# A graph network on one core: the last 14 groups of the edge layer without early products, and the last store of maxima on ScalarE's queue

## The chip, the cores and the metric

The kernel runs on one core of a Trainium2 chip. The metric is the time of one execution on the device in microseconds; the number for a kernel is the median over its runs. The chip's engines are called as in the profile: PE is TensorE (matrix products), DVE is VectorE, ACT is ScalarE, POOL is GpSimd, SP is the engine that here only issues transfers. ACT and POOL have transfer queues of their own as well. Each engine works through its instructions in a fixed order, and an instruction that waits holds up all that stand behind it on its engine.

## The reference, cut to what matters

12,500 nodes with 32 features each, 400,000 edges sorted by the node they end in (`dst`). Four graph layers follow each other, each with a residual and a layer norm. The third is the edge layer, the fourth the one behind it:

```
edge_index = jnp.stack([src, dst])
x = _layernorm(x + _L0_gnn_ref(x, src, dst, ...))
x = _layernorm(x + _L1_gnn_ref(x, edge_index, 3))
x = _layernorm(x + _L2_gnn_ref(x, edge_index, edge_attr_32, ...))   # the edge layer
x = _layernorm(x + _L3_gnn_ref(x, edge_index))                      # three rounds

# L2: rol, col = edge_index
e_feat = jnp.concatenate([x[rol], x[col], edge_attr], axis=-1)       # 96 per edge
h = jax.nn.relu(e_feat @ W1 + b1)                                    # 64
v = h @ W2 + b2                                                      # 32
x_cand = jax.ops.segment_max(v, col, num_segments=num_nodes)
return jnp.maximum(x_cand, x)

# L3, three times: msgs = norm[:, None] * x[src]; x = segment_sum(msgs, dst, n); acc = acc + x
```

## The kernel before, in words

**Matrix A.** The graph's adjacency lies in device memory as a matrix of small counts, A, in 25 blocks of columns (`NQ`) by 98 blocks of rows (`H`), with what does not fit it in an extra part, Ax. A round of the fourth layer is a product of A and Ax with x, which is split into three 16-bit parts (`x3`). In `Rounds.product` the extra part comes first (its loop value c is -1): two loads of Ax (L363, 3136 KB each), 392 matmuls on them (L377), a scan and a sum, and then the blocks of A (L354 or L363, L382).

**The edge layer** (`edge_layer`) takes the edges that are left for it in three stages, cut by node (`HS` = 52 and 78 of 98 row blocks). A stage is a chain of batches of at most 48 columns of 128 edges; a batch is worked off in groups of four columns. For a group, POOL gathers the rows of its source nodes (`fetch`, L111, four gathers), PE transposes them (L1751), DVE copies the result (L1753) and the indices of a group four further on (L1729, `allow`), PE makes the hidden layer (L1782, L1784, `hidden`), ACT applies relu (L1787), PE makes the outputs (L1800, `outer`; L1806 for the last column, which stands alone), and ACT copies them (L1802, L1808). POOL can run ahead of PE by four groups, for so many index tiles are released. When a batch is through, 32 scans of DVE (L1637) make running maxima, and the SP queue stores them to `scan` (L1640).

**The end of a stage** (`end`, then `done`): PE transposes the flags and the last maxima (L1656, L1659, L1672, L1677), DVE carries the maxima over the partitions (L1657 to L1674), POOL gathers the rows to mend (`fx`, L111), DVE mends them (L1684), POOL scatters them (L116) and then gathers the last row of every node's segment (`ends`, L111, one gather per block of 128 nodes: 20 in the last stage, in batches of eight, eight and four). DVE and ACT make x of each batch out of them (L1309 to L1319, `layernorm` L236 to L245, `split` L254 to L258). These are generators: `tick` takes each one step further per group, `steps` the scans.

**Early products.** As soon as a stage's nodes are done, the products of their rows of A for the first round of the fourth layer are begun (`round_part`): 25 blocks of columns, for each one or more loads of A (L1361, 832 KB), 52 or 26 matmuls (L1366) into one of two buffers `y`, a copy `ys` by ACT (L1373), a sum `z` by PE into the one buffer `z` (L284, placed seven products into the next block), and an addition into `part` by DVE (L1351). `fill` puts eight of them behind each half of a group. The products of the last 20 row blocks are not early; they come in the first round itself (`lo` = 78), behind Ax.

**What sets the order.** A scheduler lays the instructions of each engine in a fixed order, by priority in the order of writing and by when it reckons them ready; it can draw later-written work forward into gaps. Buffers of a pool that is closed are free for the next pool only when their users are through; the first buffer that Ax is loaded to lies where the tiles of A for the early products lay.

Of the kernel before, what the change touches and what calls it, by code (L numbers as in the profile page):

```python
# [22 lines left out]
P = 128  # L23
D = 32
# [96 lines left out]
def dense_path(ctx, tc, bad_i, x, src, dst, edge_attr, w1T, w1_b, w2, w2T, w2_b, aT,  # L121
               m_W1, m_b1, m_W2, m_b2, out):
    nc = tc.nc
# [3 lines left out]
    C = E // P  # L127
# [17 lines left out]
    HE = P * HC  # L145
    ROW = D + 2
    scan = dram.tile([E - HE, D], F32, name="scan")
# [66 lines left out]
    cuts = [HC]  # L214
# [461 lines left out]
    with ExitStack() as build:  # L676
# [15 lines left out]
        for k in (1, 256, 255):  # L692
            t = keys.tile([P, P], BF16, name=f"ident{k}")
# [273 lines left out]
        steps = []  # L967
# [324 lines left out]
    with ExitStack() as st:  # L1292
# [5 lines left out]
        fillers = []  # L1298
# [78 lines left out]

        begun = set()

        def fill(i):  # L1380
            for _ in range(2 - i):
                next(first[0], None)
            if fillers:
                k = 8 if fillers[0] in begun else 40
                begun.add(fillers[0])
                while fillers and k:
                    try:
                        next(fillers[0])
                        k -= 1
                    except StopIteration:  # L1390
                        fillers.pop(0)
# [155 lines left out]
def edge_layer(ctx, tc, ident, cuts, heads, edge_attr, m_W1, m_b1, m_W2, table, scan, starts_d,  # L1547
# [11 lines left out]
    nc = tc.nc  # L1559
    E = edge_attr.shape[0]  # L1560
    C = E // P
    HE = P * cuts[0]
    T = 48
    AHEAD = 4
    LEAD = 2 * AHEAD
    HID = m_W1.shape[1]

    const = ctx.enter_context(tc.tile_pool(name="e_const", bufs=1))
# [3 lines left out]
    def of_stage(ap, s, skip=0):  # L1572
        return ap[P * cuts[s] - skip:P * cuts[s + 1] - skip].rearrange(
            "(p t) d -> p (t d)" if len(ap.shape) == 2 else "(p t) -> p t", p=P)

    rows = const.tile([P, C], I32, name="rows")
    for s in range(len(cuts) - 1):
        nc.sync.dma_start(rows[:, cuts[s]:cuts[s + 1]], of_stage(rows_d, s))
    mw1 = const.tile([3 * D, HID], F32, name="mw1")
    mb1 = const.tile([2 * HID, 1], F32, name="mb1")  # L1580
# [14 lines left out]
    class Batch:  # L1595
# [37 lines left out]
        def maxima(self):  # L1633
            n = self.n
            prev = self.before.o[:, self.before.n - 1, :] if self.before else low
            for f in range(D):
                nc.vector.tensor_tensor_scan(self.o[:, :n, f], self.keepb[:, :n], self.v[:, :n, f],  # L1637
                                             prev[:, f:f + 1], OP.min, OP.max)
                yield
            nc.sync.dma_start(of_stage(scan, self.s, HE)[:, self.t0 * D:(self.t0 + n) * D],  # L1640
                              self.o.rearrange("p t d -> p (t d)")[:, :n * D])
            if self.t0 + n == cuts[self.s + 1] - cuts[self.s]:
                later.append(end(self.s, self.o[:, n - 1, :]))

# [3 lines left out]
    def end(s, last):  # L1648

        cont0, single, fix, _ = heads[s]  # L1650
        g = small.tile([D, P], F32, name="cg", bufs=1)
        a = small.tile([D, P], F32, name="ca", bufs=1)
        b = small.tile([D, P], F32, name="cb", bufs=1)
        c = small.tile([D, P], F32, name="cc", bufs=1)
        pr = scratch()
        nc.tensor.transpose(pr[:D], cont0.to_broadcast([P, D]), ident)  # L1656
        nc.vector.tensor_copy(g, pr[:D])  # L1657
        pr = scratch()
        nc.tensor.transpose(pr[:D], single.to_broadcast([P, D]), ident)  # L1659
        nc.vector.memset(a[:, 0:1], 0.0)  # L1660
        nc.vector.tensor_mul(a[:, 1:], g[:, 1:], pr[:D, :P - 1])
        for r in (g, a):
            nc.vector.tensor_scalar(r, r, -0.5, BIG, op0=OP.add, op1=OP.mult)
            nc.vector.tensor_scalar_mul(r, r, 2.0)
        nc.vector.memset(b[:, 0:1], -BIG)
        if s:
            nc.sync.dma_start(b[:, 0:1], scan[P * cuts[s] - HE - 1:P * cuts[s] - HE, :].rearrange(
                "o d -> d o"))
            nc.vector.tensor_tensor(b[:, 0:1], b[:, 0:1], g[:, 0:1], op=OP.min)
        yield  # L1670
        pf = scratch()
        nc.tensor.transpose(pf[:D], last, ident)  # L1672
        nc.vector.tensor_tensor(b[:, 1:], pf[:D, :P - 1], g[:, 1:], op=OP.min)
        nc.vector.tensor_tensor_scan(c, a, b, -BIG, OP.min, OP.max)  # L1674
        yield
        po = scratch()
        nc.tensor.transpose(po[:, :D], c, ident[:D, :D])  # L1677
        carry = small.tile([P, D], F32, name="carry", bufs=1)
        nc.scalar.copy(carry, po[:, :D])
        yield from range(LEAD)  # L1680
        fx = small.tile([P, D], F32, name="fx", bufs=1)
        gather(nc, fx, scan[:P * cuts[s + 1] - HE], fix)
        yield from range(2)
        nc.vector.tensor_tensor(fx, fx, carry, op=OP.max)  # L1684
        yield
        scatter(nc, scan[:P * cuts[s + 1] - HE], fix, fx)
        yield
        yield from done(s)
# [8 lines left out]
    def batch(i):  # L1697
        s, t0, n = plan[i]
        return Batch(i, s, t0, n, made[-1] if t0 else None)
# [4 lines left out]
    todo = []  # L1704

    def steps(k):
        while todo and k:
            try:
                next(todo[0])
                k -= 1  # L1710
            except StopIteration:
                todo.pop(0)

    def tick():
        for g in list(later):
            try:
                next(g)
            except StopIteration:
                later.remove(g)

    groups = [(cuts[s] + t, min(4, t0 + n - t)) for s, t0, n in plan
              for t in range(t0, t0 + n, 4)]
# [11 lines left out]
    for _ in range(AHEAD):  # L1734
        allow()
    made.append(batch(0))
    for i in range(len(plan)):
        B = made[i]
        for _ in B.ready:
            pass  # L1740
        if i + 1 < len(plan):
            made.append(batch(i + 1))
            todo.append(made[-1].ready)
        for t in range(0, B.n, 4):
            k = min(4, B.n - t)
            for j in range(k):
                B.fetch(t + j)
            allowed.pop(0)
            pT = psum.tile([P, 4, P], F32, name="pT", bufs=2)
            for j in range(k):  # L1750
                nc.tensor.transpose(pT[:3 * D, j, :], B.ef[:, t + j, :], ident)  # L1751
            eT = small.tile([3 * D, 4, P], F32, name="eT")
            behind = nc.vector.tensor_copy(eT[:, :k], pT[:3 * D, :k])  # L1753
            with tc.issue_after(behind.ins):
                allow()
            fill(0)
            stage1.append((B, t, k, eT))
            if len(stage1) > 1:
                stage2.append(hidden(nc, psum, small, mw1, mb1, *stage1.pop(0)))
            if len(stage2) > 1:  # L1760
                ready = stage2.pop(0)
                outer(nc, psum, mw2, *ready)
                if ready[1] + ready[2] == ready[0].n:
                    todo.append(ready[0].maxima())
            fill(1)
            steps(6)
            tick()
    stage2.append(hidden(nc, psum, small, mw1, mb1, *stage1.pop(0)))
    for ready in stage2:
        outer(nc, psum, mw2, *ready)  # L1770
    todo.append(B.maxima())
    steps(10 ** 6)
    while later:
        tick()


def hidden(nc, psum, small, mw1, mb1, B, t, k, eT):
# [691 lines left out]
```

## Time and profile before

| what | us |
| --- | --- |
| median of 9 runs (lowest, highest) | 7677.07 (7664.44, 7686.70) |
| the profiled execution's own time | 7678.94 |
| its span, first to last instruction | 7677.0 |
| PE busy | 6633.4 (86%) |
| DVE busy | 3924.4 (51%) |
| POOL busy | 3575.2 (47%) |
| ACT busy | 1636.3 (21%) |
| early products (L1366, 1950 of them), first to last start | 5586.4 to 6580.6 |
| gathers of the edge layer (`ef`, 2817 of them), last start | 6537.1 |
| gathers of ends of the last stage, first to last start | 6581.9 to 6605.9 |
| products of Ax in the first round (L377, 392 of them), first to last start | 6592.1 to 6638.5 |

Times in views are microseconds from the start of the span. A line of a timeline gives the start, the duration, the engine, the line of the kernel, what is written and read, how often, and in brackets how long the engine stood idle before it and what ended that. "issue" is time in which the profile shows no wait. PE's matmuls are pipelined, so a group's duration reaches a little beyond the start of the next. The granted clock is 1.00 when PE runs at full rate.

### The profile page before, as it was taken

What the parts mean: (1) busy time and instruction counts of PE and PEld (TensorE: products, weight loads), DVE (VectorE), ACT (ScalarE), POOL (GpSimd) and SP (SyncE); (2) the same over time, 40 slices, a digit from 0 to 9 for tenths busy, and PEclk for the clock granted to TensorE, in tenths of its full rate; (3) what the DMA queues carried; (4) which work ended last, traced back from release to release, by engine and by line L of the source; (5) the groups of instructions that cost most, each with busy time, mean ns of one, the idle gap of its engine ahead of it and who ended that gap; (6) DMA issues with size and microseconds to landing.
All of it is one profiled execution on the core that took longest, in us unless ns stands there. A gap on an engine that the chain in (4) does not pass through costs nothing. (4 is left out here: it accounts for less than half of the span.)

```text
span 7677.0 us, 194318 instructions
## 1 busy us (share of the span) xinstructions
PE 6633.4 (86%) x84402; PEld 5276.4 (69%) x84402; DVE 3924.4 (51%) x10962; ACT 1636.3 (21%) x3386; POOL 3575.2 (47%) x3459
## 2 busy tenths in 40 slices
PE   6778999899999988888888888778669979899998
PEld 4678899889999985555545555334335635799998
DVE  6989899561555565555555555433344333411121
ACT  1324688200000002222222222211112212100000
POOL 1002501000665727777777777777777777100000
PEclk7879999999999996777777777555559968999999
DMA  2128544799999982222222222121127735699998
GB/s 51 58 103 326 199 205 196 294 337 368 356 378 358 369 328 75 61 55 59 55 58 61 55 55 59 52 60 49 50 74 226 250 89 183 245 347 365 359 363 311
DMA packets 574338, 1447.42 MB, mean 189 GB/s; under 512 B 108023, under 2 KB 269407, under 8 KB 560031
## 3 DMA queue, kind: packets, MB, share of 16 engines
q1 hardware_dynamic: 432816, 1347.10, 47.6%
q0 software_dynamic: 109792, 66.25, 4.2%
q10 hardware_dynamic: 30864, 21.54, 1.0%
q8 instruction: 664, 10.88, 0.6%
q14 instruction: 202, 1.65, 0.1%
HBM read 1155.33 MB, written 279.27 MB: 187 GB/s over the span
## 5 line engine op out<-in xcount | busy, mean ns | idle before, releaser
L111 POOL DMA_INDIRECT ef<-table,ids x2817 | 2670.6, 948 | 883.9 <-issue 652.8
L382 PE MATMUL y<-x,a 128*128 128x96 bf16 x49980 | 2215.3, 207 | 86.2 <-issue 84.9
L382 PEld LDWEIGHTS <-a 128*128 128x128 fp8e4 x49980 | 2154.9, 98 | 117.4 <-issue 115.3
L1751 PE MATMUL pT<-ident,ef 128*96 128x128 f32 x2817 | 773.2, 356 | 586.2 <-DMA ef<-table,ids 571.0
L1751 PEld LDWEIGHTS pT<-ident,ef 128*96 128x96 f32 x2817 | 396.4, 160 | 1045.2 <-DMA ef<-table,ids 718.4
L1753 DVE COPY eT<-pT 96x512 f32<-96x512 f32 x705 | 476.3, 676 | 1045.6 <-PE pT L1751 1045.5
L1019 PE MATMUL pa<-oh,ol 128*128 128x196 bf16 x4928 | 736.4, 273 | 126.1 <-DVE oh L1009 80.6
L1800 PEld LDWEIGHTS pv<-mw,hT 128*128 128x128 f32 x3208 | 594.3, 259 | 265.1 <-issue 90.2
L1025 ACT ACTIVATE at<-pa 128x784 uint16<-128x784 f32 x816 | 646.9, 824 | 510.8 <-PE pa L1019 482.3
L1800 PE MATMUL pv<-mw,hT 128*128 128x64 f32 x3208 | 674.7, 348 | 22.1 <-ACT hT L1787 15.5
L1787 ACT ACTIVATE hT<-ph,mb 128x256 f32<-128x256 f32 x802 | 380.5, 474 | 1313.7 <-PE ph L1784 1286.3
L1019 PEld LDWEIGHTS <-ol 128*128 128x128 bf16 x4928 | 560.2, 150 | 142.0 <-issue 77.1
L1055 PE MATMUL y<-x,at 128*128 128x102 bf16 x9604 | 640.6, 210 | 9.6 <-DVE x L258 5.4
L1782 PE MATMUL ph<-eT,mw 96*64 96x256 f32 x1410 | 622.3, 534 | 11.7 <-DVE eT L1753 10.3
L278 DVE TENSOR_REDUCE v<-y 128x128 f32<-128x384 f32 (+2 forms) x152 | 83.4, 549 | 1064.4 <-PE y L272 579.5
L1784 PE MATMUL ph<-eT,mw 96*64 96x256 f32 x1408 | 625.1, 537 | 0.0
L1009 DVE TENSOR_TENSOR oh<-bins_h,pl 128x1568 bf16<-128x1568 bf16 x616 | 603.5, 980 | 0.0
L111 POOL DMA_INDIRECT g<-code_d,ws_i x25 | 215.9, 8636 | 808.4 <-DVE ki L793 589.1
L116 POOL DMA_INDIRECT sorted_d<-hrow,pos x308 | 404.3, 1313 | 379.1 <-DVE v L1249 192.3
L1055 PEld LDWEIGHTS <-at 128*128 128x128 fp8e4 x9604 | 556.9, 98 | 22.8 <-issue 11.1
L1366 PE MATMUL y<-a,x 128*96 128x512 fp8e4 (+1 forms) x1950 | 492.8, 389 | 2.3 <-DVE x L258 1.5
L1004 DVE TENSOR_TENSOR ol<-la,lb 128x1024 bf16<-128x1024 bf16 x616 | 428.0, 697 | 70.9 <-PE pa L1019 70.6
(409 smaller groups left out, 6821.4 us busy)
## 6 DMA issues: line engine op xcount, KB each, us to landing
a<-A SPq DMA_DIRECT2D x245, 3136.0 KB
A<-at SPq DMA_DIRECT2D x98, 1568.0 KB
a<-A SPq DMA_DIRECT2D x144, 832.0 KB
ef<-table,ids POOLq DMA_INDIRECT x2817
starts_d<-rows SPq DMA_DIRECT2D x44, 1024.0 KB
attr<-in_edge_attr SPq DMA_DIRECT2D x57, 768.0 KB
begin<-starts_d SPq DMA_DIRECT2D x57, 768.0 KB
scan<-o SPq DMA_DIRECT2D x57, 768.0 KB
```

The lines of the kernel that those rows point to most:

```text
L111: return nc.gpsimd.indirect_dma_start(out=o, out_offset=None, in_=tab, in_offset=IndirectOffsetOnAxis(ap=idx, axis=0))
L382: nc.tensor.matmul(y[:, q, :], block(h, q - q0), x3[:, h, :3 * F], start=(q + h == first), stop=(c >= CX and q == nq - 1 and h == H - 1))
L1009: nc.vector.tensor_tensor(oh, bins_h[:, None].to_broadcast([P, 4, HJ, 2]), pairs(pl[:, t, 0, half * 64 + w0:half * 64 + w0 + 8])[:, :, Non ...
L1019: nc.tensor.matmul(pa[:, 2 * b + i, :HJ], ols[t][:, :, :, 4 * u + 2 * b + i].rearrange("p a b -> p (a b)"), ohs[t][:, 2 * u + b, :, i], st ...
L1025: nc.scalar.activation(at[:, qd, :, off:off + 8].rearrange("p h (w j) -> p h w j", w=4), pa[:, :, :HJ].rearrange("p w (h j) -> p h w j", h ...
L1055: nc.tensor.matmul(y[0][:, q, :], at[:, q - 2 * half, h, :], x3[:, h, :3 * F0], start=(q + h == 0), stop=(not EARLY <= c < CX and last and ...
L1366: nc.tensor.matmul(y[:3 * D, :nq * Q], x3[:, h, :3 * D], a[:, :nq, h - h0, :], start=(h == lo), stop=(h == hi - 1))
L1751: nc.tensor.transpose(pT[:3 * D, j, :], B.ef[:, t + j, :], ident)
L1753: behind = nc.vector.tensor_copy(eT[:, :k], pT[:3 * D, :k])
L1782: nc.tensor.matmul(ph[:HID, :ka], mw1, eT[:, :ka], start=True, stop=True)
L1784: nc.tensor.matmul(ph[HID:2 * HID, :k - 2], mw1, eT[:, 2:k], start=True, stop=True)
L1800: nc.tensor.matmul(pv[:, j].rearrange("p h d -> p (h d)"), hT[:, j, :], mw2, start=True, stop=True)
```

## The change

`fill` gets a second argument and issues early products only where it is not zero. The count of groups that are left is divided by `HOLD` = 14, so in the last 14 groups it is zero. Behind the last group the scans are no longer written in one go, but four at a time with a `fill` between, and so are the steps of `end` and `done`. The store of the very last batch of maxima, and the small load of one row of `scan` at the end of the last stage (L1667), go to ACT's queue in place of SP's.

```
-        def fill(i):
+        def fill(i, left=1):
             for _ in range(2 - i):
                 next(first[0], None)
-            if fillers:
+            if fillers and left:
                 k = 8 if fillers[0] in begun else 40
...
+    HOLD = 14
...
-            nc.sync.dma_start(of_stage(scan, self.s, HE)[:, self.t0 * D:(self.t0 + n) * D],
-                              self.o.rearrange("p t d -> p (t d)")[:, :n * D])
+            end_of_all = self.s == len(cuts) - 2 and self.t0 + n == C - cuts[self.s]
+            (nc.scalar if end_of_all else nc.sync).dma_start(
+                of_stage(scan, self.s, HE)[:, self.t0 * D:(self.t0 + n) * D],
+                self.o.rearrange("p t d -> p (t d)")[:, :n * D])
...
-            nc.sync.dma_start(b[:, 0:1], scan[P * cuts[s] - HE - 1:P * cuts[s] - HE, :].rearrange(
+            (nc.scalar if s == len(cuts) - 2 else nc.sync).dma_start(b[:, 0:1], scan[P * cuts[s] - HE - 1:P * cuts[s] - HE, :].rearrange(
...
+    total = len(groups) + AHEAD
     for i in range(len(plan)):
...
-            fill(0)
+            total -= 1
+            left = total // HOLD
+            fill(0, left)
...
-            fill(1)
+            fill(1, left)
             steps(6)
             tick()
...
     todo.append(B.maxima())
-    steps(10 ** 6)
+    while todo:
+        steps(4)
+        fill(1)
     while later:
         tick()
+        fill(1)
```

Behind `edge_layer`, `while fillers: fill(0)` still writes what is left of the early products, before the rounds begin.

## The prediction

> **What bounds the kernel now.** I read first the busy shares (PE 86%), then the windows around the end of the edge layer, then in the timelines what TensorE (PE), GpSimd (POOL) and the SP queue do there, then the SP queue's waits. The change touches only the stretch from about 6486 us on. Before and after it the order of every engine's instructions stays, but for one small load at 6229 us.
>
> Windows (start:end, length, busy time and count of PE, PEld, DVE, ACT, POOL, then granted clock, DMA share, GB/s):
>
> ```profile
> 6404.00:6487.00 83.00, 83.00 (x492) 52.72 (x490) 26.69 (x103) 17.42 (x40) 58.74 (x63) 1.00 0.69 215
> 6487.00:6538.00 51.00, 51.00 (x304) 32.61 (x303) 15.16 (x58) 10.16 (x24) 34.87 (x37) 1.00 0.69 215
> 6538.00:6581.00 43.00, 42.91 (x254) 27.55 (x252) 11.46 (x52) 7.61 (x19) 1.94 (x3) 1.00 0.60 189
> 6581.00:6592.00 11.00, 0.63 (x4) 0.52 (x4) 0.22 (x1) 0.37 (x1) 7.62 (x9) 0.63 0.91 340
> 6592.00:6619.00 27.00, 9.31 (x94) 8.77 (x94) 14.16 (x48) 2.84 (x9) 11.50 (x12) 0.63 0.58 210
> ```
>
> PE is full until 6581 (early products, L1366, between the groups' work), then nearly idle while POOL gathers the segment ends; DMA loads in that gap. The timelines (start, duration, engine, instruction, count, idle before it and what ended that) of POOL, PE and the SP queue:
>
> ```profile
> 6537.07 0.94 POOL L111 DMA_INDIRECT ef<-table,ids  x1 [0.36 <-DVE ids L1729]
> 6576.00 0.94 POOL L111 DMA_INDIRECT fx<-scan,fix  x1 [37.99 <-DMA a<-A]
> 6579.53 0.98 POOL L116 DMA_INDIRECT scan<-fx,fix  x1 [2.59 <-DVE fx L1684]
> 6581.94 0.96 POOL L111 DMA_INDIRECT ends<-scan,end_i  x1 [1.43 <-DMA scan<-fx,fix]
> ```
>
> ```profile
> 6558.15 0.27 PE L1751 MATMUL pT<-ident,ef 128*96 128x128 f32 x1
> ...
> 6564.36 0.41 PE L1806 MATMUL pv<-mw,hT 64*128 64x32 f32 x2
> ...
> 6565.79 7.09 PE L1366 MATMUL y<-a,x 128*96 128x512 fp8e4 x32
> ...
> 6578.66 2.25 PE L1366 MATMUL y<-a,x 128*96 128x256 fp8e4 x19
> ...
> 6592.12 7.14 PE L377 MATMUL y<-a,x 128*96 128x128 fp8e4 x78 [10.06 <-issue]
> ...
> 6619.07 19.61 PE L377 MATMUL y<-a,x 128*96 128x128 fp8e4 x298 [1.41 <-DVE x L258]
> ```
>
> ```profile
> 6570.82 0.33 SPq L1640 DMA_DIRECT2D scan<-o  x1
> 6572.91 0.37 SPq L1361 DMA_DIRECT2D a<-A  x1
> 6581.05 0.98 SPq L363 DMA_DIRECT2D a<-Ax  x2
> ```
>
> And of the SP queue's waits:
>
> ```profile
> SPq L363 <- PE y L1366: 4.4, 1, 4.4
> ```
>
> To be seen: (1) PE transposes the last column 21 us after POOL gathered it (6537.07, 6558.15): PE carries a backlog. (2) The load of Ax (L363) starts when the last early product has ended (6578.66 + 2.25 = 6580.9; issue 6581.05), and its first product L377 stands 11.2 us behind that end. Today these 11.2 us lie beside the gathers of the ends, for 298 of the 392 products of Ax wait for the last x at 6619.0. They end at 6638.7, and the round behind them cannot start sooner.
>
> **The change, part by part.** I follow one chain: P, the end of the last early product, then the load of Ax, then L377.
>
> *No products in the last 14 groups.* The first group held is transposed at 6485.7. In the changed order 35 of the 298 products left then still stand between the last nine groups, and 263 stand behind t0, the end of the last group's L1806. Before, t0 = 6564.8, with 72 behind it.
> - POOL is freed of its waits for ids. The next gather starts at 6487.40; 36 follow before the last at the pace of 6164 to 6240 (1.249 us each): 6532.3, against 6537.1 (no gain).
> - From there to t0: a landing of 2.4 us (the scatter of 6579.53, its reader at 6581.94). Then, before, 6.6 us from 6558.15 to t0, with 18 products at 0.216 (the row of 32: 6565.79 to 6572.71), 3.9; without them 2.7, with the 7 left 4.2; at half clock twice that, 8.4. The stretch without products, 6200 to 6250, ran at 0.50, one with 5 or 6 per group at 0.72 to 0.74: I take 6. PE's lag there is 0 to 5; I take 2, as from 6200 to 6250 PE was busy for 37.7 of 50 us and POOL waited for nothing. t0 = 6542.8 (6539 to 6548).
>
> *The small load of a column (L1667)* goes from SP to ScalarE's queue around 6229; what it waits for lands by 6229.3 and ScalarE's neighbours stand at 6229.5 and 6231.2: nothing.
>
> *The last store of maxima on ScalarE.* Before, SP issues it at 6570.82, when the 32 scans end at 6570.8: SP held nothing back. On ScalarE's queue a copy ys (L1373) stands ahead of it, which needs 29 products and a z (0.81): 29 x 0.216 + 0.8 + 0.6 = 7.7 us behind t0, against 6.1. So it comes 1.7 us later relative to t0, and with it the gather of fx. TensorE's four transposes of the carry, too, stand behind 53 products and two z: 13.6 us, against 10.6. From t0 to the first gather of ends it was 17.2; I take 20 (17.2 to 22.7, the upper with a landing under load: 6600.91 to 6607.12, 6.2 us).
> The Trainium skill ("Trainium Kernel Development and Optimization", Key Constraints) says that DMAs from all queues share the same 16 DMA engines, and that another issuing engine only saves issue time. By it this edit is worth at most the row's 0.33 us; without the ys copy ahead the sum would be about 1.7 us lower.
>
> *Ends.* 20 gathers: 23.97 from the first's start to the last's (6581.94, 6605.91), and a landing of 2.4 (to 6.2): 26.4. So the last batch lands at 6542.8 + 20 + 26.4 = 6589.2; x is ready 9.3 later (6609.75 to 6619.02), at 6598.5, 20.5 earlier than now.
>
> *A new wait.* In the changed order ScalarE's copy ys of one block of columns stands behind L257 of the first batch of ends, and that (over L256) behind VectorE's L1309 of the third batch, so behind the last gather's landing. z of that block (L284) waits for this ys. PE reaches it 34.8 us behind t0 (140 products 30.3, five z 4.0, four transposes 0.5); the copy ends 46.4 + 2.0 behind t0 (L1309 0.34, L256 0.43, L257 0.41, ys 0.58, gaps). PE stands still for some 13 us, everything queued behind that z: 97 full products, 26 half ones (0.118), five z: 21.0 + 3.1 + 4.0 = 28.1. Resuming cold costs up to 3 (at 6619 the clock is 0.50 for 5.9 us); I take 2.5. P = 6589.2 + 2.0 + 30.6 = 6621.8, against 6580.9.
>
> *Load of Ax, then L377.* Its wait for the last product stays. Nothing covers it now: 11.2 to the first product. 196 of the first half: 65 in 5.9 us at half clock, 131 at 0.05, 12.5; the second half lands 8 us behind the first and takes 9.8. End: 6621.8 + 33.5 = 6655.3, against 6638.7: 16.6 later. The tiles of A behind it come in beside L377, as now, so the rest shifts as a whole.
> The page "TensorE: Matmul & The Clock Gate", Part 1, has the clock released after some 3.4 us of activity. The row says 5.9. By the page both cold starts together would cost about 2 us less, and the sum would be +14.5.
>
> **Sum.** The profiled execution spans 7677.0 us (device time 7678.9, 1.9 above the median 7677.1). Its span plus 16.6 is 7693.6; on the median, 7693.7. With all lower values P = 6539 + 17.2 + 26.4 + 2 + 28.1 = 6612.7, +7.5; with all upper ones 6548.2 + 22.7 + 30.2 + 2 + 31.1 = 6634.2, +29.
>
> **Rivals.**
> - *Faster: x sets the end, not the products.* If the load of Ax could start ahead of the last product, L377 would start at x, 20.5 us earlier: 7656.6. For it: the critical chain now runs over x. Against it: the SP wait above. It decides if the products end by 6589.8 (6638.7 - 15.4 - 33.5); their bare PE time behind t0, 237 x 0.216 + 26 x 0.118 + ten z + transposes = 63, forbids that unless t0 is below 6527, ahead of the last gather.
> - *No new wait.* If ys is not held up, P = t0 + 63 + 1.5 = 6607.3, end 6640.8, +2: 7679. For it: ys is ready early. Against it: ScalarE's order.
> - *The tiles of A starve PE.* Products back to back need 832 KB in 2.8 us, 297 GB/s; the rows above moved 215. At 215 a tile takes 3.9 us: 1.1 more on four tiles ahead of the carry and on nine behind the wait, +14, together +31: 7708. For it: gathers and store share the DMA engines. Against it: 32 products ran without a gap at 6565.79.
>
> **How the numbers follow.** 0.2% (15.4 us) is about what a measurement of this kernel can tell from no change. My case 0.65, of which 0.50 above that bound and 0.15 below; starved 0.16; no new wait 0.10; faster 0.09. So slower 0.66, same 0.25, faster 0.09. The range reaches from near the case without the wait to near the starved one, 7680 to 7707; what is left out is the faster case and the tails.
>
> **What would show it.** Right: the last gather of ef near 6532, ends gathered from about 6563; some 10 us or more of PE idle ahead of a z L284 that waits for ys; last L1366 near 6622 and L363 directly behind it; L377 starting 11 us later, after x is long ready, ending near 6655. Wrong: L363 issued while products still run, no gap at L284, or a last product before 6600. What would upset the sum most: PE's clock in the held groups, and the landing of store and gathers while tiles stream.

## The result, and the profile after

The changed kernel takes 7700.11 us, the median of 10 runs (7692.48 to 7706.98), against 7676.26 for the kernel before on the same chip (30 runs, 7664.18 to 7689.12). The ratio is 1.0031, 95% interval 1.0023 to 1.0039: 24 us slower. The forecast was 7693.7, slower, with a range of 7680 to 7707.

The profiled execution of the changed kernel spans 7687.8 us (device time 7689.7), some 10 us less than its median. It runs ahead of the kernel before's by about 11 us from 2700 us on, long before the change: the same scatter of `starts_d` stands at 2685.03 and at 2673.77. So absolute times of the two pages can't be set side by side. I use two marks. The first is the gather of `ef` that is the 53rd from the last, the first gather of the first held group; it is POOL's, and the change has not touched anything by then. It stands at 6464.67 before and at 6454.17 after. The second is t0, the end of the last column's output (L1806 before, L1815 after). From the first mark to the end of the products of Ax (L377) it is 174.0 us before and 196.9 after: 22.9 longer. Behind that end the changed kernel is 1.6 shorter (1036.7 against 1038.4). 22.9 - 1.6 = 21.3 is what these two executions differ by behind the mark; the medians differ by 24.

Windows of the changed kernel's profile from t0 = 6532.06 on (start:end, length, busy time and count of PE, PEld, DVE, ACT, POOL, then granted clock, DMA share, GB/s):

```profile
6532.00:6568.00 36.00, 35.34 (x185) 21.95 (x184) 8.88 (x46) 3.28 (x7) 11.09 (x12) 1.00 0.82 258
6568.00:6585.00 17.00, 0.00 (x0) 0.00 (x0) 8.29 (x25) 1.31 (x4) 9.95 (x11) 0.55 0.20 60
6585.00:6616.00 31.00, 30.76 (x163) 20.62 (x163) 7.56 (x30) 4.33 (x11) 0.00 (x0) 0.91 0.54 165
6616.00:6627.00 11.00, 0.81 (x7) 0.60 (x6) 0.22 (x1) 0.37 (x1) 0.00 (x0) 0.73 0.88 341
6627.00:6651.00 24.00, 24.00 (x395) 24.00 (x396) 0.00 (x0) 0.00 (x0) 0.00 (x0) 0.91 0.87 332
```

TensorE works 36 us on early products, does nothing at all for 17, works another 31, waits 11 for Ax, and then does all 392 products of Ax in one piece. In the 17 empty microseconds the DMA engines are at 0.20 and 60 GB/s, so tiles of A are not what it waits for. What it waits for shows in the timelines of TensorE (PE) and ScalarE (ACT) (start, duration, engine, instruction, count, idle before it and what ended that):

```profile
6561.98 5.79 PE L1366 MATMUL y<-a,x 128*96 128x512 fp8e4 x26
6585.24 1.92 PE L284 MATMUL z<-S,ys 96*128 96x32 f32 x8 [17.47 <-DVE ln_s L237]
...
6613.87 2.25 PE L1366 MATMUL y<-a,x 128*96 128x256 fp8e4 x19
...
6626.95 24.12 PE L377 MATMUL y<-a,x 128*96 128x128 fp8e4 x392 [9.68 <-DMA a<-Ax]
```

```profile
6559.91 0.58 ACT L1373 COPY ys<-y 96x512 f32<-96x512 f32 x1 [5.86 <-PE y L1366]
6578.13 0.21 ACT L243 ACTIVATE ln_s<-ln_s 128x8 f32<-128x8 f32 x1 [17.64 <-DVE ln_s L242]
...
6584.30 0.41 ACT L257 CAST x<-rest 128x256 bf16<-128x256 f32 x1 [3.73 <-DVE rest L256]
6584.61 0.57 ACT L1373 COPY ys<-y 96x512 f32<-96x512 f32 x1
```

The product of the block ended at 6567.8, but its copy `ys` runs at 6584.61, directly behind L257 of the first batch of ends. In its brackets the profile names L237 of VectorE as what ended the idle time; but the z reads `ys`, whose copy ends at 6585.18, 0.06 ahead of it. And L257 waits, over L256, for L1309 of the third batch, that is for the last gather of ends.

VectorE's timeline shows this, and a second wait that lies inside the same gap:

```profile
6577.56 0.46 DVE L1309 TENSOR_TENSOR ends<-ends,rest 128x256 f32<-128x256 f32 x1 [4.41 <-DMA ends<-scan,end_i]
...
6579.52 0.28 DVE L1351 TENSOR_TENSOR part<-part,z 128x128 f32<-128x128 f32 x1
...
6583.64 0.29 DVE L1309 TENSOR_TENSOR ends<-ends,rest 128x128 f32<-128x128 f32 x1 [3.13 <-DMA ends<-scan,end_i]
6583.85 0.42 DVE L256 TENSOR_TENSOR rest<-ends,x 128x256 f32<-128x256 f32 x1
```

L1351 at 6579.52 is the addition of the z before (6561.16). There is one buffer `z`, so the z that waits can't begin before this addition has read it, at 6579.80; and on VectorE the addition stands behind L1309 of the second batch, that is behind another landing. So VectorE's order would have held TensorE up for the first 12.0 of the 17.5 us even with `ys` ready. ScalarE's copy is what ends last, and adds the other 5.4.

The stages on POOL, and the load of Ax on SP:

```profile
6521.84 0.94 POOL L111 DMA_INDIRECT ef<-table,ids  x1 [0.30 <-issue]
...
6543.85 0.94 POOL L111 DMA_INDIRECT fx<-scan,fix  x1 [21.07 <-DMA scan<-o]
6551.27 0.98 POOL L116 DMA_INDIRECT scan<-fx,fix  x1 [6.48 <-DVE part L1351]
6556.09 0.96 POOL L111 DMA_INDIRECT ends<-scan,end_i  x1 [3.84 <-DMA scan<-fx,fix]
```

```profile
6616.26 0.97 SPq L363 DMA_DIRECT2D a<-Ax  x2
```

The last early product ends at 6616.1 and Ax is issued 0.14 later, as before; but x has been ready since 6592.9, so now nothing lies beside the 10.8 us to the first product of Ax.

### The profile page after: what moved, and what is told of

Same layout as the page of the kernel before. It is cut to its first block, busy times and chain, and to the rows that moved or that the text cites. A ratio compares the mean times of both kernels' runs of the same rounds, so it can differ in the third digit from the quotient of the medians.

```text
span 7687.8 us, 194314 instructions
## 1 busy us (share of the span) xinstructions
PE 6647.5 (86%) x84402; PEld 5278.3 (69%) x84402; DVE 3924.5 (51%) x10962; ACT 1636.0 (21%) x3386; POOL 3571.4 (46%) x3459
## 5 line engine op out<-in xcount | busy, mean ns | idle before, releaser
L1055 PE MATMUL y<-x,at 128*128 128x102 bf16 x9604 | 643.8, 210 | 10.2 <-DVE x L258 6.0
L1055 PEld LDWEIGHTS <-at 128*128 128x128 fp8e4 x9604 | 560.3, 98 | 23.7 <-issue 11.8
L1366 PE MATMUL y<-a,x 128*96 128x512 fp8e4 (+1 forms) x1950 | 497.9, 393 | 1.9 <-DVE x L258 1.1
```

The costliest lines, as they stand in the source:

```text
L1055: nc.tensor.matmul(y[0][:, q, :], at[:, q - 2 * half, h, :], x3[:, h, :3 * F0], start=(q + h == 0), stop=(not EARLY <= c < CX and last and ...
L1366: nc.tensor.matmul(y[:3 * D, :nq * Q], x3[:, h, :3 * D], a[:, :nq, h - h0, :], start=(h == lo), stop=(h == hi - 1))
```

## The experiments

**The table.** All times are from each run's profiled execution: m is the first gather of the first of the 14 groups (the first mark above), t0 the end of the last column's output, "ends" the first gather of ends, "x" the end of the last L258, P the end of the last early product, E the end of the products of Ax. Ratios are against runs of the kernel before on the same chip. The times are those of one execution each and the ratios those of the medians, so the two need not agree to a few microseconds.

| kernel | ratio (95%) | m to t0 | t0 to ends | t0 to x | t0 to P | t0 to E | m to E |
| --- | --- | --- | --- | --- | --- | --- | --- |
| before | 1 | 100.1 | 17.2 | 54.3 | 16.1 | 73.9 | 174.0 |
| changed | 1.0031 (1.0023, 1.0039) | 77.9 | 24.0 | 60.8 | 84.1 | 119.0 | 196.9 |
| e5, 14 held, ends' work behind products | 1.0005 (0.9996, 1.0014) | 77.8 | 20.9 | 81.0 | 63.8 | 98.6 | 176.4 |
| e6, 7 held | 1.0011 (1.0000, 1.0022) | 84.6 | 23.7 | 62.5 | 58.0 | 92.5 | 177.1 |
| e7, 7 held, ends' work behind products | 1.0000 (0.9990, 1.0010) | 84.9 | 23.6 | 64.5 | 41.5 | 83.0 | 167.9 |
| e8, 4 held | 0.9997 (0.9988, 1.0006) | 85.3 | 26.0 | 65.8 | 31.7 | 84.5 | 169.7 |
| e9, 4 held, scans in one go | 0.9981 (0.9972, 0.9991) | 85.3 | 21.0 | 59.5 | 31.1 | 76.4 | 161.7 |
| e10, Ax doesn't wait for products | 1.0010 (1.0000, 1.0019) | 80.5 | 24.8 | 74.2 | 81.9 | 105.5 | 186.0 |
| e11, changed, scans in one go | 1.0026 (1.0016, 1.0035) | 80.6 | 20.8 | 56.5 | 80.8 | 116.4 | 197.0 |
| e12, e7 with scans in one go | 0.9993 (0.9984, 1.0002) | 85.8 | 24.0 | 64.6 | 41.7 | 83.1 | 168.9 |

The first four runs (e1 to e4) are not in it: they fell on a chip on which the kernel before takes 8939 us, and where ScalarE and VectorE stop in the middle of the edge layer for something that the profile calls "remote". The last 1400 us of the profiles of the kernel before, the changed one, e5 and e9 hold no such stop.

### The two parts by themselves: queue (e1) and held products (e2)

e1 is the kernel before with

```
-            nc.sync.dma_start(of_stage(scan, self.s, HE)[...], self.o...)
+            (nc.scalar if end_of_all else nc.sync).dma_start(of_stage(scan, self.s, HE)[...], self.o...)
...
-            nc.sync.dma_start(b[:, 0:1], scan[...])
+            (nc.scalar if s == len(cuts) - 2 else nc.sync).dma_start(b[:, 0:1], scan[...])
```

> The kernel before with nothing but the two moves to ScalarE's queue (the last store of maxima and the small load of one row of scan); all early products stay where they were. Theory (the loss comes from the products that now stand behind the last group and from a wait on ScalarE there; the queue is no part of it): in the kernel before, the copy ys that stands ahead of the store on ScalarE ends at 6570.74, when the scans end too (6570.8), so the store goes out at the same time: 7676, ratio 1.000 within 0.0005. Rival (the store behind ScalarE's copies costs what I counted for it, 1.7 us and more, or lands later from this queue): 7679 to 7682, ratio 1.0004 to 1.0008.

Measured: ratio 0.9997 (0.9984 to 1.0010). From t0 the store goes out at 6.06 (6.06 before), the gather of `fx` at 11.15 (11.24), the first gather of ends at 17.18 (17.18). The interval alone would allow the rival's 1.0004 to 1.0008; it is these times that show that the queue by itself moves nothing, as the theory had it.

e2 is the changed kernel with both transfers on `nc.sync` again.

> The changed kernel with the store and the small load back on SP's queue. Theory: on SP the store stands behind four loads of A whose buffers come free one by one as the products behind the last group run, so it goes out about as late (about 6.5 to 7 us behind the last column's output, against 7.3 on ScalarE), and the wait of z for ScalarE's copy stays: 7699, ratio 1.0030, within 2 us of the changed kernel. Rival (the late store and what follows from it is the main loss, because it delays the gather of ends and so the end of the wait): 7690 or less, ratio 1.0018 or less.

Measured: ratio 1.0027 (1.0016 to 1.0039). The store goes out 7.8 behind t0 (7.3 in the changed kernel), and TensorE stands still 18.2 us ahead of the same z. So the whole loss is there without the queue. On SP's queue, between tiles of A, the gather of `fx` comes 8.1 behind the store (4.5 in the changed kernel), and the gathers of ends begin at 25.0 instead of 24.0: beside tiles of A the queue may be worth 1 us, which one execution on this chip does not settle. That both come out as expected is worth more for the order of events than for the sizes, as the chip is the slower one.

### Taking the wait away (e3, e4, e5)

e3 and e5 are one kernel. All early products are written before the ends, and the work of ScalarE and VectorE on the ends is queued behind the last `ys` and the last addition into `part`. `issue_after` queues what its block writes behind one instruction on that instruction's engine; TensorE's order stays the same word for word.

```
+            while s == len(HS) and fillers:
+                fill(0)
             todo = []
...
+                if s == len(HS):
+                    with tc.issue_after(last_of[0].ins), tc.issue_after(last_of[1].ins):
+                        ends_to_x(h0, k, e)
+                    return
...
-                    nc.vector.tensor_add(o, o, z[:, :k])
+                    last_of[1] = nc.vector.tensor_add(o, o, z[:, :k])
...
-                nc.scalar.copy(ys[:3 * D, :nq * Q], y[:3 * D, :nq * Q])
+                last_of[0] = nc.scalar.copy(ys[:3 * D, :nq * Q], y[:3 * D, :nq * Q])
```

(`ends_to_x` holds the same instructions as `finish`, from L1309 to `split`.)

> The changed kernel, but ScalarE's and VectorE's work on the ends of the last stage is queued behind the last copy ys and the last addition into part of the early products; TensorE's order stays word for word. So no copy ys waits for a gather of ends, but x is made only when the products are through. Theory (the wait of z for ys stops TensorE for some 17 us): no gap ahead of a z; the products end 64 us behind the last column's output, at 6606.6 on the time scale of the kernel before; VectorE needs some 17 to 19 us for x behind that, the last 298 products of Ax 17 to 20: end near 6644, 5 later than before, 7682, ratio 1.0007 (7679 to 7687). Rival 1 (the tiles of A, or the late load of Ax alone, set the pace, and the wait merely lies beside them): the products end no earlier than in the changed kernel, x still comes behind them, 7700 to 7710. Rival 2 (x made late costs as much as the wait saves): no gap, but 7698 or more.

Measured in e3: ratio 1.0033 (1.0020 to 1.0046), a gap of 14.3 us ahead of the same z, outside what the theory allowed. But the copy it waited for had nothing of the program ahead of it; this is ScalarE's line of it in the timeline:

```profile
7848.99 0.58 ACT L1391 COPY ys<-y 96x512 f32<-96x512 f32 x1 [20.98 <-remote]
```

Its input was ready at 7835.3. A stop of that kind has taken the place of the wait, so e3 decides nothing, and the same kernel went to the chip again as e5.

> The kernel of e3 once more (ends' work of ScalarE and VectorE behind the last copy ys and the last addition into part). In e3 ScalarE stood still for 21 us ahead of one copy ys with nothing that the program makes it wait for (the profile names 'remote'); such stops are all over the profiles of e1 to e4, whose kernel before took 8939, and the profiled kernel before of 7677 has none in its last 1400 us. So e3 told nothing. Theory (z waits for ys because ScalarE's order puts the ends ahead of it): without such stops no gap ahead of any z, last early product 64 to 67 us behind the last column's output (84 in the changed kernel), the products of Ax end 100 to 104 behind it (119), ratio 1.0007 (1.0003 to 1.0014). Rival (the gap only covers something else, code or tiles of A, that then ends last): a gap of 10 us or more elsewhere on TensorE, ratio 1.0025 or more.

Measured in e5: ratio 1.0005 (0.9996 to 1.0014), from the mark to E 176.4. TensorE's timeline around the z that was late (L1384 is L1366 here, L1391 is L1373):

```profile
6569.89 5.79 PE L1384 MATMUL y<-a,x 128*96 128x512 fp8e4 x26
6575.51 0.98 PE L284 MATMUL z<-S,ys 96*128 96x32 f32 x8
6576.32 5.82 PE L1384 MATMUL y<-a,x 128*96 128x512 fp8e4 x26
...
6601.59 2.25 PE L1384 MATMUL y<-a,x 128*96 128x256 fp8e4 x19
...
6614.64 24.08 PE L377 MATMUL y<-a,x 128*96 128x128 fp8e4 x392 [9.64 <-DVE rest L240]
```

The z that begins at 6575.51 stands 35.4 behind t0 and waits for nothing; in the changed kernel it stood at 53.2. The products end at 63.8 instead of 84.1, and from the mark to E it is 20.5 less. The ratios say the same: 1.0031 to 1.0005 is 0.0026, 20 us. So the gap, and the clock that is lost by it, is nearly all of the loss. But e5 moves the work of both engines, ScalarE's and VectorE's. By the lines above, moving ScalarE's alone would have left 12 of the 17.5 us; no run tried that. What is left, 2.4 us on the marks, is about what the prediction's rival without the wait had (+2).

e4 took away the waiting instructions instead of the order. It leaves out the copies `ys`, the sums `z` and the additions into `part` for the blocks of columns 20 to 24 of the last early part, so these sums are missing in its output.

```
+        FROM = 20
...
+                if s == len(HS) - 1 and c >= FROM:
+                    continue
                 ys = wk.tile([P, CH], F32, name="ys")
```

> The changed kernel without the copies ys, the sums z and the additions into part of the last five blocks of columns (20 to 24) of the last early part; these sums are left out of the computation, all products stay. It takes away what waits, and leaves ScalarE's and VectorE's order on the ends as it is. Theory: no gap of TensorE; the products end some 60 us behind the last column's output (64 less five z of 0.81), at 6602.5, the load of Ax still begins there, its products 11 us later, and they need 23 us: end near 6636, 3 earlier than before, 7674, ratio 0.9996 (7670 to 7679). Rival 1 (the tiles of A set the pace, not the wait): the products' end comes only the 4 us of the five z earlier, 7696. Rival 2 (what counts is only that Ax is loaded after the last product, whenever x is ready): the same as the theory, so this run does not tell it apart; the next runs do.

Measured: ratio 1.0031 (1.0018 to 1.0044), a miss. The run was badly cut: the z that waits is the one of block 19, which stays; TensorE stood 4.1 us ahead of it, and another 7.1 in three stops ahead of it with nothing named. On that chip it tells nothing of the price, and e5 has answered the question.

### How many groups (e6, e8)

`HOLD = 7` and `HOLD = 4` in place of 14, nothing else.

> The changed kernel with 7 groups held instead of 14. 184 products behind the last column's output instead of 263. Theory (end = the later of last product + 11 + 24 and x + 19.6; a copy ys still stands behind the ends' work on ScalarE, now the one two blocks before the last): last column's output near 6545 on the scale of the kernel before, first gather of ends 23 later, last landing 6595, the gap of TensorE ends at 6598, last product 6602, end 6638: as before, ratio 1.000 (0.9993 to 1.0007). Rival 1 (the loss grows with the groups held, in proportion): half of it, 1.0015. Rival 2 (x sets the end): 6624, 14 earlier, 0.9982.

> 4 groups held, nothing else differs from the changed kernel. By the program's order every copy ys now stands ahead of the ends' work on ScalarE. Theory: the last column's output 14 us earlier than before (64 products of 0.216), near 6551; the carry behind 67 products more, so the first gather of ends 27 behind it; last landing 6604, x 6614, end 6633: 5 earlier than before, ratio 0.9993 (0.9986 to 1.0000). Rival 1 (in proportion to the groups held): 1.0009. Rival 2 (backlog of TensorE does not matter for the gathers): x and end as before, 1.0000.

Measured: e6 1.0011 (1.0000 to 1.0022), m to E 177.1, 3 above before where the theory had 1 below, and the ratio lies outside the expected range, a miss; e8 0.9997 (0.9988 to 1.0006), m to E 169.7, 4.3 below before. In proportion to the groups it would have been 11.5 and 6.5 above. For e8 the ratio rules that out as well (1.0009 expected by it); for e6 it doesn't (1.0015), and only the marks of one execution speak against it. The gap is there with 7 groups too, 13.4 us ahead of the second last z, and with only 19 half products behind it:

```profile
6585.51 1.92 PE L284 MATMUL z<-S,ys 96*128 96x32 f32 x8 [13.44 <-DVE ln_s L237]
6587.23 4.27 PE L1366 MATMUL y<-a,x 128*96 128x256 fp8e4 x19
```

With 4 groups every `ys` stands ahead of the ends' work, there is no gap, and P is long past when x comes. There it is the carry that is late. VectorE's line of e8 that joins it to `fx`:

```profile
6566.49 0.19 DVE L1687 TENSOR_TENSOR fx<-fx,carry 128x32 f32<-128x32 f32 x1 [1.39 <-ACT carry L1682]
```

That is 21.9 behind t0 (14.3 before): the change writes eight products behind every four scans, so the carry's transposes come behind some 80 products.

### Seven groups without the gap (e7, e12)

e7 is e5 with `HOLD = 7`.

> 7 groups held, and the ends' work of ScalarE and VectorE behind the last copy ys and the last addition, as in e5. Theory: no gap; the last product at 6587, ahead of the landing of the second batch of ends (6591), so x is hardly later for it (6605); 298 products of Ax behind x: end 6625, 13 earlier than before, ratio 0.9983 (0.9978 to 0.9990). Rival (the products behind the last group cost by themselves, or x becomes late by the order as it does with 14 groups): 1.000 or more.

Measured: ratio 1.0000 (0.9990 to 1.0010), a miss: no gap, P at 41.5 as expected, but m to E 167.9 where 160 was meant. t0 came 84.9 behind the mark and not 81, and x 64.5 behind t0 and not 60: VectorE begins with the ends only behind the last addition, waits 5.5 us for the second batch with one step of the first done, and does the rest of all three batches in one piece. Of the 6.1 us gained up to E, 2.6 are given back behind it (E to the end of the span 1040.9, against 1038.4); e8, e9 and e12 give back 2 to 4 in the same way, while in the changed kernel, e5 and e6 this stretch is 1.6 to 3.3 shorter than before. What makes the difference was not followed further.

e12 adds to e7 what e9 (below) changes in the order of writing, and queues the first batch of ends only behind the addition of block 22.

```
-    while todo:
-        steps(4)
-        fill(1)
+    steps(10 ** 6)
```

> 7 groups held, scans in one go, the ends' work queued behind the additions as in e7, but of the first batch only behind the addition of block 22. Theory (x alone sets the end: the last product is through 41 us behind the last column's output): gathers of ends from 18 to 20 behind it (23.6 in e7), x ready 56 behind it (64.5 in e7), products of Ax end 75 to 77 behind it (83.0): from the 53rd gather from the last 160, against 174.0 before and 167.9 in e7, 2 to 3 us given back behind: ratio 0.9984 (0.9978 to 0.9992), faster than both kernels. Rival (what x gains is lost again, since Ax and its tiles of A come no earlier): 0.9995 or more.

Measured: ratio 0.9993 (0.9984 to 1.0002), m to E 168.9, a miss by 9. The carry was early (12.3 behind t0, against 19.7 in e7), but the transfers it meets were slow, as these two lines of POOL show:

```profile
6569.39 0.98 POOL L117 DMA_INDIRECT scan<-fx,fix  x1 [5.25 <-DVE fx L1709]
6574.75 0.96 POOL L112 DMA_INDIRECT ends<-scan,end_i  x1 [4.37 <-DMA scan<-fx,fix]
```

From the store to the gather of `fx` it took 6.4, from there to its use 5.5, from the scatter to the gather of ends 5.4: together 17.3, where it was 5.2 + 3.1 + 2.4 = 10.7 before. The gathers of ends begin at 24.0, no earlier than in e7.

### Scans in one go (e9, e11)

The same edit as just shown, to e8 and to the changed kernel.

> As e8 (4 groups held), but the last 32 scans are written in one go again, as in the kernel before; products follow only between the steps behind them. The carry's transposes then stand behind 40 products that follow the last column's output, not 80. In e8 the gathers of ends began 26.0 behind that output, against 17.2 before. Theory (writing products between the scans delays the carry, and with it the gathers of ends and x): they begin 18 to 20 behind it, x is ready 56 to 58 behind it (65.8 in e8), the products of Ax end 8 us earlier than in e8; from a gather ahead of the change (the 53rd from the last) to that end 162, against 174.0 before and 169.7 in e8; of it 2 us are given back behind, as in e7 and e8: ratio 0.9987 (0.9980 to 0.9994). Rival (the carry waits for the store and its landing anyway): as e8, 0.9997.

> The changed kernel (14 groups held) with the last 32 scans written in one go. Theory: the carry's transposes stand behind 40 products instead of 53, the gathers of ends begin 19 to 20 behind the last column's output (24.0), so the gap ahead of z ends 4 to 5 us earlier, and with it all behind it: ratio 1.0025 (1.0018 to 1.0032). Rival (the gap's end is not set by the landing of the last ends): as the changed kernel, 1.0031.

Measured in e9: ratio 0.9981 (0.9972 to 0.9991), m to E 161.7 where 162 was expected. The carry is ready at 11.1 behind t0 (21.9 in e8) and `fx` now waits for its own gather; ends begin at 21.0, a little later than the 18 to 20 expected. TensorE's timeline of e9 at the end:

```profile
6609.48 1.06 PE L284 MATMUL z<-S,ys 96*128 96x32 f32 x4 [17.66 <-ACT ys L1373]
6612.51 6.79 PE L377 MATMUL y<-a,x 128*96 128x128 fp8e4 x94 [1.97 <-DVE part L1351]
6620.30 16.84 PE L377 MATMUL y<-a,x 128*96 128x128 fp8e4 x298 [1.00 <-DVE x L258]
```

Here x ends last again, as before the change, only 12 us sooner; and it beats both kernels, the one before by 0.19%. A gap of 17.7 us is there all the same, ahead of the very last z, whose `ys` stands behind work on the ends again. It costs next to nothing, because no early product is queued behind it and the 94 products of Ax that don't need the last x still end 1.0 us ahead of it. So in e9 the gap by itself costs nothing; in the changed kernel what costs is the work that it pushes past x.

Measured in e11: ratio 1.0026 (1.0016 to 1.0035), gathers of ends at 20.8 and the gap ends at 48.8 instead of 53.2, nearly as expected; E is 2.7 earlier behind t0, but t0 is 2.7 later behind the mark, so that from the mark nothing is gained (197.0). The interval doesn't exclude the changed kernel's 1.0031, so the place of the gap's end is shown, and the gain in time is not.

### The load of Ax (e10)

14 groups, no copy behind a landing (the ends' work of each batch is queued behind the additions of blocks 19, 20 and 21), and the pools of the rounds opened so that the first load of Ax doesn't lie on tiles of A:

```
-            self.ap = st.enter_context(tc.tile_pool(name="ap", bufs=3))
             self.accp = st.enter_context(tc.tile_pool(name="accp", bufs=1))
+            self.acc = self.accp.tile([P, H, D], F32, name="acc")
+            self.ap = st.enter_context(tc.tile_pool(name="ap", bufs=3))
...
-            self.acc = self.accp.tile([P, H, D], F32, name="acc")
```

> 14 groups held, no copy ys behind a landing of ends (the ends' work of each batch is queued behind that addition into part which comes just before its landing), and the pools of the rounds opened in another order, so that the first load of Ax goes to memory where the batches of the edge layer lay, not the early products' tiles of A: it waits for the transposes of the carry, no longer for the last early product. To be held against e5 (ratio 1.0005), where the load began 0.1 behind the last product and its first product 10.7 later. Theory (the uncovered load is the rest of the loss): last product 64 to 68 behind the last column's output, all 392 products of Ax directly behind it, their end 85 to 89 behind it (98.6 in e5): from the 53rd gather from the last 163 to 167, against 176.4 in e5; ratio 0.9988 (0.9980 to 0.9996). Rival (Ax loaded earlier takes the DMA engines from the tiles of A, and the products end as much later): 1.0003 or more.

Measured: ratio 1.0010 (1.0000 to 1.0019), m to E 186.0, 9.6 more than e5: the rival. (The profiled execution is the slowest of its 11 runs, 12.7 us above their median; the medians put e10 only some 4 us above e5, within the noise, so the 9.6 may be too much.) Ax was issued 12.9 and 23.3 behind t0 and its first product stands 1.5 behind P, so the 11 us are gone. But two windows of e10, and TensorE's lines in them (L1387 is L1366), show what they were paid with:

```profile
6559.00:6588.00 29.00, 22.98 (x119) 14.37 (x119) 8.87 (x46) 2.69 (x6) 4.89 (x6) 0.91 0.87 302
6588.00:6605.00 17.00, 11.58 (x49) 6.54 (x49) 0.29 (x1) 0.58 (x1) 13.04 (x14) 0.80 1.05 364
```

```profile
6588.18 9.02 PE L1387 MATMUL y<-a,x 128*96 128x512 fp8e4 x33 [5.47 <-DMA a<-A]
...
6604.57 6.55 PE L1387 MATMUL y<-a,x 128*96 128x512 fp8e4 x20 [5.25 <-DMA a<-A]
```

The DMA engines are busy throughout the second window (a share of 1.05), and TensorE waits 10.7 us for tiles of A that stand behind Ax on the same queue. The 33 and 20 products behind these gaps take 1.9 and 2.2 longer than at 0.216 each, and three copies `ys` are now 0.73 late each, as the scheduler laid the products out anew. 10.7 + 4.1 + 2.2 = 17.0; P came 18.2 later than in e5. So the uncovered load of Ax is part of the time of the changed kernel, but this edit only moves it to the tiles of A. Whether another place for Ax would do better wasn't tried.

## Why the prediction was right, and where its sizes were off

**Direction and cause.** Slower was right, and for the reason given: the copy `ys` behind L257, that behind the landing of the last ends, and TensorE held up at the one z in between. e5 removes this wait, VectorE's with it, and 20 of the 23 us. What the prediction didn't see is that VectorE's addition into `part` holds the same z up, over the one buffer `z`, until 5.4 us before `ys` is there; the copy still ends last, so the sum didn't need it. Step by step, in the prediction's own terms:

| step | predicted | measured |
| --- | --- | --- |
| mark (6464.67) to the last gather of ef | 67.6 | 67.7 |
| that gather to t0 | 10.5 | 10.2 |
| t0 to the first gather of ends | 20 (17.2 to 22.7) | 24.0 |
| gathers of ends, first to last | 23.97 | 23.97 |
| t0 to the z that waits: reached, begun | 34.8, 48.4 | 35.7, 53.2 |
| that z to P | 30.6 | 30.9 |
| P to the first product of Ax | 11.2 | 10.8 |
| products of Ax | 22.3 | 24.1 |
| t0 to E | 112.5 | 119.0 |

**Held groups.** POOL at its full pace, and the 2.4 of landing and 6 of TensorE with a lag of 2, came out within 0.3 us in sum, but by luck in the parts. From the last gather's start to its transposes it was 5.93 where the sum had 4.4, and from there to t0 4.29 where it had 6: the granted clock was 0.50 from 6505 to 6525, as feared, but 1.00 over these last 4.29 us.

**Store on ScalarE's queue.** The 7.7 behind t0 was 7.3. It goes out 1.1 us behind the end of the scans; on SP it is 1.6 (e2, on the slower chip).

**From t0 to the gathers of ends** is the term that was mis-sized, 4 us, and it lies outside the bounds that I gave. I took the carry's transposes for what comes late. They did come late (the carry is ready at 13.95, against 11.05), but nothing waited for them. What took the time is two small transfers beside the tiles of A: from the gather of `fx` to its use it took 6.75 (3.07 before), from the scatter to the gather of ends 4.82 (2.41). 1.3 of store - 0.7 of its landing + 3.7 + 2.4, and 0.2 more from the use to the scatter, give the 6.9 from 17.2 to 24.0. The single landing under load that I put into the upper bound was one of ends; I didn't see that there are two transfers in a chain here, and that both now lie beside tiles of A. From the gather of `fx` to its use the DMA engines moved 11 GB/s before and 280 after, from the scatter to the gather of ends 7 and 252. The prediction's row for this stretch covers 43 us (189 GB/s), in which the quiet moment of these two transfers doesn't show.

**The gap** was put at 13.6 and is 17.5. TensorE reaches the z 0.9 later than forecast, and the z begins 4.8 later: the 4.0 from the gathers of ends, 1.2 because the last gather lands 3.6 behind its start and not 2.4, less 0.5 in the steps up to `ys`. **Resuming cold** was put at 2.5: the z and the 26 products behind the gap take 9.0 from 6585.24 to 6594.26, and 6.4 in the next block, so 2.6. The granted clock was at half for the first 5.1 us behind the gap, and for the first 4.3 us of the products of Ax.

**The products of Ax** were put at 22.3, from rows of before; they took 24.1. The cold start was sized well: the first 65 took 5.7 us where I had 5.9. What was mis-sized is the product at full clock, 0.0558 us from start to start and not 0.05, which makes 1.9 us over the other 327. The row of 298 from before has the same 0.0558 behind its first stretch, so this could have been read there.

**The rivals.** "No new wait" is what e5 brought about: +2.4 on the marks and a ratio of 1.0005, where I had +2; E stands 98.6 behind t0, where the rival had 98.0. "Tiles of A starve PE" did not hold: 0.43 us of waiting for tiles in the whole stretch, at 258 GB/s. e10 shows that it is near: with Ax added to the same window it does. "Faster, x sets the end" needed the load of Ax to come ahead of the last product, and that it does not is the SP line of 6616.26.

**Sum.** 24 us measured against 16.6. In the two profiles it is 21.3, that is 4.7 more than forecast: 6.5 more between t0 and E, 0.2 less ahead of t0, and 1.6 less behind E, which the prediction took to be unchanged. The other 2.7 lie between these two executions and the medians.

## What to carry to other kernels

Work that is moved behind a stage is queued, on every engine that it needs, with whatever that stage's end has there; look for every copy or sum that the scheduler lays behind an instruction that waits for a transfer, because in a fixed order it stops all engines that need it. There can be several for one wait, as here on ScalarE and VectorE, and the profile's bracket names at most the last. When the amount moved is a number in the code, try small ones: 4 groups with the scans left in one piece were 0.19% faster than before where 14 groups were 0.31% slower. And a chain of small transfers has to be priced at what it takes beside the loads that will run then, each link for itself.

## What the runs showed of the hardware that I had not expected

Small transfers mostly took longer when large loads ran beside them. From the gather of `fx` to its use it took 3.07 us in the kernel before, at 11 GB/s, and 5.05 to 6.75 in the changed kernel, e5, e9, e10, e11 and e12, at 230 to 328 GB/s. From the scatter to the gather that reads behind it it took 2.41 before, at 7 GB/s, and 2.5 to 5.9 in these. The rate alone doesn't set it: in e6 and e7 the gather took 4.2 at 314 and 304 GB/s, and the scatter the old 2.4 at 168 and 170.

An early load takes its time from the loads behind it when the DMA engines are busy anyway: a share of 1.05 at 364 GB/s in e10, with TensorE waiting for tiles. 364 is no fixed ceiling: from 6627 to 6632 the changed kernel moved 419 GB/s at a share of 1.03. The Trainium skill ("Trainium Kernel Development and Optimization", Key Constraints) says that transfers of all queues share the same 16 DMA engines, and that another issuing engine only saves issue time. That a gather on POOL's queue took 6.75 instead of 3.07 beside tiles on SP's queue fits it, though no run here separates this from other causes. e1 agrees with the part that another issuing engine saves at most issue time: the first gather of ends stands at 17.18 behind t0 with either queue.

The same program can be slower by 16% on another chip: the kernel before took 8939 us on the one of e1 to e4 and 7674 to 7690 on the others. There idle times of ScalarE and VectorE of up to 28 us end with "remote", and some of TensorE of up to 22 us are put down to "issue", in the middle of the edge layer. What they waited for wasn't found.
